# A four-layer cross-attention stack: the third layer's norms and gate by exp and ln, its experts joined at the gate, its maxima's products placed between other work

## The chip, the cores and the metric

One core of one Trainium2 chip. The metric is the device time of one execution in microseconds (us), and the time of a kernel is the median of its runs.

## The reference, cut to what matters

Sixteen sequences of 56 tokens (width 256) pass through four layers, and every layer attends to the same context of 1500 rows per sequence (width 128). Layer 0 is one attention with a sigmoid gate, layers 1 and 3 are attention with 16 heads and a GELU feed-forward, and layer 2, the third one, is what changes:

```python
vm = expert_mask(token_type_ids)[..., None]              # token picks expert v or l
x = rms_norm(hidden_states, ln_in_w)
mixed = jnp.where(vm, x @ v_qkv, x @ l_qkv)              # then causal self attention
hidden_states = residual + jnp.where(vm, ctx @ v_dense, ctx @ l_dense)
ci = rms_norm(hidden_states, ln_post_cross_w)
cq = heads(ci @ cq_w, NH, CHD)                           # 16 heads of 8
ck, cv = jnp.split(encoder_outputs @ ckv_w, 2, axis=-1)  # 1500 keys
cctx = sdpa(cq, ck, cv, causal=False)
hidden_states = hidden_states + cctx @ cdense_w
mi = rms_norm(hidden_states, ln_post_attn_w)
v_out = jax.nn.silu(mi @ v_gate) * (mi @ v_up) @ v_down
l_out = jax.nn.silu(mi @ l_gate) * (mi @ l_up) @ l_down
hidden_states = hidden_states + jnp.where(vm, v_out, l_out)
```

Inputs and results are fp32.

## The kernel before

The sixteen sequences form four groups of four (224 tokens, two tiles of 112). The program is a list of sixteen items, layer by layer and group by group: items 0 to 3 are layer 0, 4 to 7 layer 1, 8 to 11 layer 2, 12 to 15 layer 3. Of every item the attention over the context runs in front (`att0`, `att13`, `att2`), and beside it, as a Python generator `side` that is advanced one step at a time between the attention's rounds, run the end of the item before (`post...`: output projection, feed-forward) and the start of the item after (`pre...`: norm, projections, and in layer 2 the self attention). A scheduler then puts each engine's instructions in order by program order, priorities and its own estimates; each engine works through its own queue in that fixed order.

**Layer 2's cross attention** (`att2`) counts half sequences n = 0 to 31, eight for each group. Each has six rounds (`NR`), a round being 250 of the 1500 keys. For half sequence n a round does, on TensorE: `weights(n, r + 1)`, four products (L984) into two PSUM banks, of which ScalarE takes the exponential (L991, two instructions); and `sums(n, r)`, four products with the values (L1012). The softmax needs each row's maximum first, so `maxima(n + 1)` runs one half sequence ahead: twelve **links**, two in each round. A link is two products (L941) into one of two banks and a VectorE maximum over that bank (L947). Two links that follow each other use the two banks in turn, so the third link's products wait until the first link's maximum has been read out. After the twelfth link comes the **tail**: the maximum over the links (L950), a split into two parts (L952, L953), a TensorE transpose (L955) and a spread copy (L961), which `weights(n + 1, 0)` needs. `att2` advances the generator `look` of the links at set points of a round (`next(look, None)`), and runs its rest and the tail at the fourth round with raised priority; nothing fixes where the scheduler puts a link among the other products.

**Keys and values** (`keys_values`) of the next sequence are made in the same rounds, one step for every second half sequence: GpSimd subtracts neighbouring key blocks (L874, L875: one instruction over 1250 columns) and spreads the queries (L888: one over 896 columns), TensorE multiplies (L895, L904).

**Norms**: `rms_rstd` squares on ScalarE (L258), takes the square root there (L260), and the reciprocal on VectorE (L261); then come the scaling (L269) and the transposes (L220). It is used twice in `pre2`, once in `post2`, and in layer 0. ScalarE evaluates functions out of one loaded table, and an ACT_TABLE_LOAD stands in its queue wherever the next function is not in it: Exp, Sqrt and Silu are in three different ones, copies and squares in all.

**The feed-forward** (`post2`) goes expert by expert. The normed rows come twice, once masked for expert v and once for l. For each expert the whole gate and up weights are loaded (`load_w`, three buffers `w`), and for each of six column tiles gate and up products (L1152) share a bank, Silu reads it (L1156), VectorE multiplies (L1157). The down products (L1166) of both experts add up in one bank.

The link's code, and where a round advances it:

```python
for r in range(NR):
    for i, bank in enumerate(cross["scores"]):
        ...                      # two products (L941), one maximum (L947)
        yield
```

## Time and profile before

| what | value |
|---|---|
| median of three runs (lowest, highest) | 2965.62 us (2954.15, 2970.51) |
| the profiled execution: its own time, its span | 2950.62 us, 2948.8 us |
| busy: PE, PEld, DVE, ACT, POOL | 2756.1, 2035.4, 1497.3, 1257.6, 123.1 us |
| mean granted TensorE clock, whole span | 0.979 |
| layer 2's cross attention, 1084 to 2024 us: PE, DVE, ACT busy, clock | 811.27, 477.67, 392.76 of 940 us, 0.95 |
| layer 1 with its neighbours, 450 to 980 us: PE busy, clock | 528.77 of 530 us, 1.00 |
| layer 3, 2100 to 2948 us: PE busy, clock | 838.79 of 848 us, 1.00 |

PE is TensorE's matmuls, PEld its weight loads, DVE VectorE, ACT ScalarE, POOL GpSimd. A wait row reads "engine line <- engine line: us in total, times, longest"; a timeline row gives start, length, engine, line, operation, operands, how many, and in brackets the idle time ahead of it with what ended it.

### The profile page before, as it was taken

How to read it: one execution, taken by the hardware profiler on the slowest of the kernel's cores; microseconds unless marked ns; L12 is line 12 of the kernel's file. 1: busy time of each engine (PE TensorE's matmuls, PEld its weight loads, DVE VectorE, ACT ScalarE, POOL GpSimd, SP SyncE). 2: the span in 40 equal slices, each digit the busy share in tenths (PEclk: the TensorE clock that was granted, in tenths of full speed). 3: DMA queues.
4: the chain of work that ended last, by engine and by line, in shares of the span. 5: the costliest groups of instructions: out<-in, count | busy, mean ns of one | idle time of the engine just before them, and what ended most of it. 6: DMA issues, size and time to landing. Idle time of an engine off the chain costs nothing.

```text
span 2948.8 us, 39063 instructions
## 1 busy us (share of the span) xinstructions
PE 2756.1 (93%) x15546; PEld 2035.4 (69%) x15546; DVE 1497.3 (51%) x3660; ACT 1257.6 (43%) x2098; POOL 123.1 (4%) x118
## 2 busy tenths in 40 slices
PE   5899999999999999888888988989999999999998
PEld 3677777777777766556566655756777777777777
DVE  2445645546546544654455465355455555555553
ACT  1444444444444433346235334535345345344443
POOL 0000000000000000010001000000000000000000
PEclk8999999999999999999989989999999999999999
DMA  5221121121110133253324423441211111111100
GB/s 171 97 77 38 34 81 37 35 81 37 35 60 24 53 92 89 53 128 102 74 72 114 117 53 82 116 116 54 91 43 58 56 37 63 56 37 49 56 22 4
DMA packets 72139, 198.47 MB, mean 67 GB/s; under 512 B 7334, under 2 KB 39718, under 8 KB 71958
## 3 DMA queue, kind: packets, MB, share of 16 engines
q1 hardware_dynamic: 71958, 195.98, 23.0%
q8 instruction: 123, 2.02, 0.3%
q14 instruction: 58, 0.48, 0.1%
HBM read 145.88 MB, written 0.92 MB: 50 GB/s over the span
## 4 chain that ended last, share of the span: by engine, by line
PE 83%; DVE 10%; ACT 3%; issue 2%; DMA 1%; SPq 1%; DVEq 0%; ACTq 0%
PE o L344 19%; PE sc L305 19%; PE t L332 9%; PE o L1012 6%; DVE mx L947 3%; PE sc L941 3%; PE mm L1152 2%; PE t L984 2%; PE mm L690 2%; PE mm L661 2%; PE mm L571 2%; PE mm L677 2%; PE mm L1166 1%; PE t L593 1%; PE sc L904 1%
## 5 line engine op out<-in xcount | busy, mean ns | idle before, releaser
L344 PE MATMUL o<-pt,kv 125*128 125x256 f32 (+1 forms) x3072 | 661.2, 357 | 5.5 <-DVE pt L339 1.6
L344 PEld LDWEIGHTS o<-pt,kv 125*128 125x128 f32 x3072 | 519.9, 190 | 201.7 <-ACT pt L213 68.8
L305 PE MATMUL sc<-kt,qa 128*128 128x500 f32 x1344 | 635.2, 587 | 0.7 <-ACT qa L213 0.5
L314 DVE CUSTOM_DVE_ANT_0 p<-sc,mb 128x500 f32<-128x500 f32 x672 | 448.2, 673 | 214.2 <-PE sc L305 206.0
L321 ACT ACTIVATE p<-p,few 128x1500 f32<-128x1500 f32 x224 | 346.1, 1545 | 303.3 <-DVE few L319 302.7
L213 ACT ACTIVATE pt<-t 125x512 f32<-125x512 f32 x464 | 264.7, 590 | 374.1 <-PE t L332 351.8
L332 PEld LDWEIGHTS t<-ident,p 128*125 128x125 f32 x2688 | 356.8, 187 | 56.2 <-issue 15.4
L332 PE MATMUL t<-ident,p 128*125 128x128 f32 x2688 | 370.0, 273 | 2.1 <-DVE p L323 1.9
L947 DVE TENSOR_REDUCE mx<-sc 112x2 f32<-112x500 f32 x384 | 251.3, 674 | 200.4 <-PE sc L941 199.9
L305 PEld LDWEIGHTS sc<-kt,qa 128*128 128x128 f32 x1344 | 225.3, 190 | 135.3 <-issue 100.0
L991 ACT ACTIVATE pt<-t 125x448 f32<-125x448 f32 x384 | 192.3, 541 | 252.8 <-PE t L984 251.1
L339 DVE COPY pt<-t 125x512 f32<-125x512 f32 x224 | 154.3, 689 | 238.1 <-PE t L332 237.6
L941 PE MATMUL sc<-k,qs 128*112 128x250 f32 x768 | 188.9, 343 | 61.2 <-DVE mx L947 59.9
L323 DVE TENSOR_SCALAR p<-p,few 128x1500 f32<-128x1500 f32 x224 | 228.0, 1018 | 5.1
L941 PEld LDWEIGHTS sc<-k,qs 128*112 128x112 f32 x768 | 113.7, 184 | 123.8 <-DVE mx L947 88.7
L1012 PE MATMUL o<-pt,vc 125*64 125x224 f32 x1536 | 197.4, 387 | 0.3
L984 PE MATMUL t<-qs,k 128*125 128x224 f32 x768 | 146.0, 286 | 2.0 <-ACT pt L991 2.0
L322 DVE RECIPROCAL few<-few 128x1 f32<-128x1 f32 x224 | 36.0, 161 | 205.3 <-ACT p L321 205.3
L1012 PEld LDWEIGHTS o<-pt,vc 125*64 125x64 f32 x1536 | 101.1, 144 | 46.6 <-ACT pt L991 3.2
L984 PEld LDWEIGHTS t<-qs,k 128*125 128x125 f32 x768 | 120.1, 195 | 9.8 <-issue 4.0
L213 ACT ACTIVATE ot<-o 128x256 f32<-128x256 f32 (+1 forms) x128 | 45.4, 354 | 177.6 <-PE o L344 177.5
L120 POOL TENSOR_SCALAR mb<-m 128x1500 bf16<-128x1500 uint8 x32 | 46.9, 1465 | 1757.8 <-DVE few L314 1353.9
(272 smaller groups left out, 2724.2 us busy)
## 6 DMA issues: line engine op xcount, KB each, us to landing
kt<-in_ctxT SPq DMA_DIRECT2D x48, 750.0 KB
kv<-in_ctx SPq DMA_DIRECT2D x38, 750.0 KB
k<-kh SPq DMA_DIRECT2D x128, 187.5 KB
k<-kl SPq DMA_DIRECT2D x128, 187.5 KB
w<-in_L_W SPq DMA_DIRECT2D x16, 1024.0 KB
w<-in_L_Wq SPq DMA_DIRECT2D x8, 1024.0 KB
w<-in_L_Wo SPq DMA_DIRECT2D x8, 1024.0 KB
m<-in_mask_k SPq DMA_DIRECT2D x32, 187.5 KB
```

The source lines that it names most:

```text
L213: nc.scalar.activation(out, in_, AF.Copy, scale=scale)
L305: nc.tensor.matmul(sc[:n, :SW], qa[:, off : off + n], kt[:, cols], start=True, stop=True)
L314: nc.vector.tensor_tensor_reduce(p[:n, cols], sc[:n, :SW], mask[:n, cols], 1.0, LOWEST, ALU.add, ALU.max, mx[:n, s : s + 1],)
L321: nc.scalar.activation(p[:n], p[:n], AF.Exp, bias=nm[:n], accum_out=den[:n])
L323: nc.vector.tensor_scalar(p[:n], p[:n], den[:n], None, ALU.mult)
L332: nc.tensor.transpose(t[:CP, j * gw + off : j * gw + off + n], p[:n, c * CP : (c + 1) * CP], ident[:n, :n],)
L344: nc.tensor.matmul(o[:, :gw], kv[:, c, :], pt[:, j * gw : (j + 1) * gw], start=(c == 0), stop=(c == NC - 1),)
L941: nc.tensor.matmul(sc[:, e], made["q"][:, g, 2 * e : 2 * e + 2, :].rearrange("p h n -> p (h n)") .bitcast(F32R), k.bitcast(F32R), start=(r ...
L947: nc.vector.tensor_reduce(mx[:, 2 * i : 2 * i + 2, r], sc, AX.X, ALU.max)
L984: product = nc.tensor.matmul(t[:, i * T : (i + 1) * T], made["k4"][g][:, c * CP : (c + 1) * CP].bitcast(F32R), made["q"][:, g].rearrange(" ...
L991: nc.scalar.activation(pt[:, : 2 * T], t, AF.Exp)
L1012: av = nc.tensor.matmul(o[i * 64 : (i + 1) * 64, half * T : (half + 1) * T], made["v"][:, at : at + 64], pts[h][:, i * T : (i + 1) * T], s ...
```

## The change

Line numbers above and below are those of the kernel before. The change has six parts:

- `rms_rstd(x, ln=True)` in layer 2 takes Ln and then Exp with scale -0.5 in place of the square root, and one Newton step by five small VectorE instructions in place of the reciprocal.
- `post2` adds both experts' gate products in one bank (each token's rows are zero for the other expert), and likewise the up products. Silu becomes Exp, Ln, Exp on ScalarE and a VectorE product with the gate. Weights are loaded in halves of the columns, both experts in one buffer; the down products of the two experts go to two halves of a bank, and four VectorE instructions per group add them, weighted with the new table `takes`. That table is made once, at the end of layer 0's first item, by eight one-column products, a copy and one more instruction.
- Beside item 9 a table that holds both Exp and Ln is loaded ahead.
- GpSimd's subtraction runs in five instructions of 250 columns, its spread in four of 224.
- `maxima` yields ahead of a link instead of behind it, and each link is given the name of an instruction that its products must follow on TensorE (`look.send`, `behind`: an order, not a wait): the last of the next weights' products or the last of the sums' products.
- The points of a round at which `att2` advances the links move to behind `weights` and behind `sums`. Their number in a round stays.

```diff
...
@@ -188,6 +190,16 @@
         nc.vector.memset(vm, 0.0)
         nc.vector.tensor_mul(vm[:, :, : N - 1], is1v[:, :, : N - 1], is1v[:, :, 1:])
         nc.vector.tensor_scalar(nvm, vm, -1.0, 1.0, ALU.mult, ALU.add)
+
+        nc.vector.memset(share, 1.0 / 128)
+        p = mm()
+        vmf = vm.rearrange("p b n -> p (b n)")
+        for i in range(B * N // TP):
+            nc.tensor.matmul(
+                p[:TP, i : i + 1], vmf[:, i * TP : (i + 1) * TP], share, start=True, stop=True
+            )
+        nc.vector.tensor_copy(takes[:, 0], p[:TP, : B * N // TP])
+        nc.vector.tensor_scalar(takes[:, 1], takes[:, 0], -1.0, 1.0, ALU.mult, ALU.add)
@@ -251,19 +263,31 @@
             )
         return xT
-    def rms_rstd(x):
+    def rms_rstd(x, ln=False):
         ss = stat(NT)[:TP]
         sq = xpool.tile([TP, NT, D], F32, tag="xn", name="sq")
         for i in range(NT):
             nc.scalar.activation(sq[:, i, :], x[:, i, :], AF.Square, accum_out=ss[:, i : i + 1])
         rstd = stat(NT)[:TP]
-        nc.scalar.activation(rstd, ss, AF.Sqrt, bias=eps6[:TP], scale=1.0 / D)
-        nc.vector.reciprocal(rstd, rstd)
+        if ln:
+
+            nc.scalar.activation(rstd, ss, AF.Ln, bias=eps6[:TP], scale=1.0 / D)
+            nc.scalar.activation(rstd, rstd, AF.Exp, scale=-0.5)
+
+            v, t = stat(NT)[:TP], stat(NT)[:TP]
+            nc.vector.tensor_scalar(v, ss, 1.0 / D, 1e-6, ALU.mult, ALU.add)
+            nc.vector.tensor_mul(t, rstd, v)
+            nc.vector.tensor_mul(t, t, rstd)
+            nc.vector.tensor_scalar(t, t, -0.5, 1.5, ALU.mult, ALU.add)
+            nc.vector.tensor_mul(rstd, rstd, t)
+        else:
+            nc.scalar.activation(rstd, ss, AF.Sqrt, bias=eps6[:TP], scale=1.0 / D)
+            nc.vector.reciprocal(rstd, rstd)
         return rstd
     def rmsnorm_T(x, w, gi, masked):
-        rstd = rms_rstd(x)
+        rstd = rms_rstd(x, True)
         xn = xpool.tile([TP, NT, D], F32, tag="xn", name="xn")
         for i in range(NT):
             nc.vector.tensor_scalar(
@@ -351,6 +375,14 @@
         for _ in steps:
             pass
+    def behind(ins, name, why):
+
+        tc.add_manual_dep(
+            ins, name,
+            mybir.DependencyInfo(mybir.DependencyClass.NoSync, mybir.DependencyReason.DATA),
+            reason=why,
+        )
+
@@ -872,9 +904,10 @@
         else:
             kd = wpool.tile([128, 2048], F32, tag="w", name="kd")[:, :M]
         nc.gpsimd.tensor_copy(kd[:, : 2 * CP], kt[:, : 2 * CP])
-        nc.gpsimd.tensor_tensor(
-            kd[:, 2 * CP :], kt[:, 2 * CP :], kt[:, : M - 2 * CP], ALU.subtract
-        )
+        for c in range(2 * CP, M, 2 * CP):
+            nc.gpsimd.tensor_tensor(
+                kd[:, c : c + 2 * CP], kt[:, c : c + 2 * CP], kt[:, c - 2 * CP : c], ALU.subtract
+            )
         kh, kl = (big.tile([128, 2 * R], F32, tag="qa", name=n)[:, :M] for n in ("kh", "kl"))
         made["k"] = kh, kl
         vc = kpool.tile([CP, KV], F32, tag="kv", name="vc")
@@ -885,10 +918,11 @@
         qs = mpool.tile([128, 4, 4, N], F32, tag="mb", name="qs")
         made["q"] = qs
         cq = state["cq"][:, :, b % G * N : (b % G + 1) * N]
-        nc.gpsimd.tensor_tensor(
-            qs.bitcast(F32R), cq.unsqueeze(2).to_broadcast([128, 4, 4, N]),
-            m_four.unsqueeze(1).unsqueeze(3).to_broadcast([128, 4, 4, N]), ALU.mult,
-        )
+        for g in range(4):
+            nc.gpsimd.tensor_tensor(
+                qs[:, g].bitcast(F32R), cq[:, g].unsqueeze(1).to_broadcast([128, 4, N]),
+                m_four.unsqueeze(2).to_broadcast([128, 4, N]), ALU.mult,
+            )
         for s in range(NS):
             p = bank()
             cols = slice(s * SW, (s + 1) * SW)
@@ -933,19 +967,22 @@
         mx = small.tile([TP, 4, NR], F32, tag="mx", bufs=2, name="mx")
         for r in range(NR):
             for i, bank in enumerate(cross["scores"]):
+                at = yield
                 sc = bank[:TP, :SW].rearrange("p (e k) -> p e k", e=2)
                 g = n % 2 * 2 + i
                 k = made["k4"][g][:, r * 2 * CP : (r + 1) * 2 * CP]
                 for e in range(2):
-                    nc.tensor.matmul(
+                    product = nc.tensor.matmul(
                         sc[:, e],
                         made["q"][:, g, 2 * e : 2 * e + 2, :].rearrange("p h n -> p (h n)")
                         .bitcast(F32R),
                         k.bitcast(F32R), start=(r + e == 0), stop=True, skip_group_check=True,
                     )
+                    if at:
+                        behind(product.ins, at, "links between the others' products")
                 nc.vector.tensor_reduce(mx[:, 2 * i : 2 * i + 2, r], sc, AX.X, ALU.max)
-                yield
+        yield
         nm = few(4)[:TP]
         nc.vector.tensor_reduce(nm, mx, AX.X, ALU.max, negate=True)
...
@@ -1020,6 +1049,7 @@
                     if c == 0 and half:
                         behind(av, last[i], "groups of sums in a bank")
                     last[i] = av.name
+        return av.name
     def cross_own(o, out):
@@ -1062,6 +1092,13 @@
         steps = keys_values(gi * G, state)
         return steps if gi else run(steps)
+    def none():
+        while True:
+            yield
+
+    nothing = none()
+    next(nothing)
+
     def att2(gi, state, then, side):
         x = xs[gi]
         xf = x.rearrange("p i d -> p (i d)")
@@ -1080,7 +1117,7 @@
             ask(1)
             run(maxima(0))
             looks[1] = maxima(1)
-            for _ in range(2):
+            for _ in range(3):
                 next(looks[1])
         ready = cross.pop("ready", None)
         making = iter(())
@@ -1100,26 +1137,29 @@
                 pts = ready[0]
                 if r == NR - 1 and n + 2 < end:
                     looks[n + 2] = maxima(n + 2)
-                look = looks.get(n + 1 + r // (NR - 1), iter(()))
+                    next(looks[n + 2])
+                look = looks.get(n + 1 + r // (NR - 1), nothing)
                 if r == NR - 1:
                     ready = weights(n + 1, 0) if n + 1 < end else None
                 else:
-                    next(look, None)
                     ready = weights(n, r + 1)
+                    if r < NR - 2:
+                        look.send(ready[1])
                 next(side, None)
                 if not half:
                     next(making, None)
                 if r == 2 and n + 2 < end:
                     ask(n + 2)
-                next(look, None)
                 if r % 2:
                     next(side, None)
-                sums(n, r, pts, o, last, ready[1] if r < NR - 1 else None)
+                at = sums(n, r, pts, o, last, ready[1] if r < NR - 1 else None)
+                if r != NR - 2:
+                    look.send(at)
                 if r in (0, 2, NR - 1):
-                    next(look, None)
+                    look.send(at)
                 elif r == NR - 3:
                     with tc.high_priority(offset=200):
-                        run(look)
+                        next(look, None)
             if half:
                 cross_own(o, ccT[:, :, b * N : (b + 1) * N])
         cross["ready"] = ready
@@ -1134,42 +1174,53 @@
     def post2(gi, state):
         x = xs[gi]
-        xf = x.rearrange("p i d -> p (i d)")
         xe = rmsnorm_T(x, "L2_ln_post_attn_w", gi, True)
         yield
-        hs, downs = [], []
-        for n, e in enumerate("vl"):
-            (wg,) = load_w((a[f"L2_{e}_gate"], 2, I2))
-            (wu,) = load_w((a[f"L2_{e}_up"], 2, I2))
-            hT = big.tile([128, 8, T], F32, tag="hT", bufs=2, name="h2T")
-            for f in range(NF2):
-                cols = slice(f * 128, min(I2, (f + 1) * 128))
+
+
+        hT = big.tile([128, 8, T], F32, tag="hT", bufs=2, name="h2T")
+        for f0 in (0, NF2 // 2):
+            lo, hi = f0 * 128, min(I2, (f0 + NF2 // 2) * 128)
+            kinds = [
+                load_w(*((a[f"L2_{e}_{k}"][:, lo:hi], 2, hi - lo) for e in "vl"))
+                for k in ("gate", "up")
+            ]
+            for f in range(f0, f0 + NF2 // 2):
+                cols = slice(f * 128 - lo, min(hi, (f + 1) * 128) - lo)
                 w = cols.stop - cols.start
                 p = mm()
-                for k, wt in enumerate((wg, wu)):
-                    for c in range(2):
-                        nc.tensor.matmul(
-                            p[:w, k * T : (k + 1) * T], wt[:, c, cols], xe[n][:, c, :],
-                            start=(c == 0), stop=(c == 1),
-                        )
-                nc.scalar.activation(hT[:w, f, :], p[:w, :T], AF.Silu)
+                for k, experts in enumerate(kinds):
+                    for n, wt in enumerate(experts):
+                        for c in range(2):
+                            nc.tensor.matmul(
+                                p[:w, k * T : (k + 1) * T], wt[:, c, cols], xe[n][:, c, :],
+                                start=(n + c == 0), stop=(n + c == 2),
+                            )
+                    yield
+
+                s = tmp("silu")[:w, :T]
+                nc.scalar.activation(s, p[:w, :T], AF.Exp, scale=-1.0)
+                nc.scalar.activation(s, s, AF.Ln, bias=ones[:w])
+                nc.scalar.activation(s, s, AF.Exp, scale=-1.0)
+                nc.vector.tensor_tensor(hT[:w, f, :], p[:w, :T], s, ALU.mult)
                 nc.vector.tensor_tensor(hT[:w, f, :], p[:w, T : 2 * T], hT[:w, f, :], ALU.mult)
-                yield
-            hs.append(hT)
-            downs.append(load_w((a[f"L2_{e}_down"], NF2, D))[0])
-        p = mm()
+        downs = [load_w((a[f"L2_{e}_down"], NF2, D))[0] for e in "vl"]
         for i in range(NT):
+            p = mm()
             for n in range(2):
                 for f in range(NF2):
                     w = min(128, I2 - f * 128)
                     nc.tensor.matmul(
-                        p[:TP, i * D : (i + 1) * D], hs[n][:w, f, i * TP : (i + 1) * TP],
-                        downs[n][:w, f, :],
-                        start=(n + f == 0), stop=(n == 1 and f == NF2 - 1),
+                        p[:TP, n * D : (n + 1) * D], hT[:w, f, i * TP : (i + 1) * TP],
+                        downs[n][:w, f, :], start=(f == 0), stop=(f == NF2 - 1),
                     )
                 yield
-        nc.vector.tensor_add(xf, xf, p[:TP, : NT * D])
+            for n in range(2):
+                nc.vector.scalar_tensor_tensor(
+                    x[:, i, :], p[:TP, n * D : (n + 1) * D],
+                    takes[:, n, gi * NT + i : gi * NT + i + 1], x[:, i, :], ALU.mult, ALU.add,
+                )
@@ -1188,6 +1239,11 @@
         return items[k][1](items[k][4], states[k]) if k < len(items) else None
     def beside(k):
+        if k == 2 * groups + 1:
+
+            tc.keep_in_program_order(
+                nc.scalar.preload_act_table_set("natural_log_exp_and_others")
+            )
         if k:
             _, _, _, post, gi = items[k - 1]
             yield from post(gi, states.pop(k - 1))
```

## The prediction

> **What bounds the kernel now.** I read the page first: the totals, the clock in 40 slices, and the chain that ended last.
>
> ```profile
> span 2948.8 us, 39063 instructions
> ...
> PEclk8999999999999999999989989999999999999999
> ...
> PE 83%; DVE 10%; ACT 3%; issue 2%; DMA 1%; SPq 1%; DVEq 0%; ACTq 0%
> ```
>
> TensorE is the chain, except for a tenth that is VectorE's. Windows by stage, of which two rows follow (length, then busy time of PE, PEld, DVE, ACT, POOL, then the clock), say where that tenth lies.
>
> ```profile
> 1084.00:2024.00 940.00, 811.27 (x5257) 585.00 (x5257) 477.67 (x977) 392.76 (x713) 68.53 (x74) 0.95 0.37 93
> ...
> 1276.00:1281.00 5.00, 4.50 (x19) 3.67 (x21) 2.36 (x6) 1.95 (x5) 0.10 (x1) 0.73 0.82 279
> ```
>
> Layers 1 and 3 keep PE busy for 99% at clock 1.00. Layer 2's cross attention, 940 us, leaves it idle for 129 us and at a clock of 0.95. What PE waited for in that stage, in the waits:
>
> ```profile
> PE sc L941 <- DVE mx L947: 59.9, 75, 2.0
> PE sc L955 <- DVE nml L953: 20.8, 18, 2.0
> PE mm L220 <- DVE xn L269: 12.9, 6, 2.8
> PE mm L733 <- DVE s L729: 12.2, 8, 3.3
> ...
> PE t L984 <- ACT pt L991: 2.0, 5, 0.5
> ```
>
> Half of it is the links waiting for an earlier maximum; ScalarE, whose queue holds many table loads, is hardly waited for. One such link in the timeline:
>
> ```profile
> 1248.75 1.02 PE L941 MATMUL sc<-k,qs 128*112 128x250 f32 x4
> 1249.60 0.49 PE L984 MATMUL t<-qs,k 128*125 128x224 f32 x3
> 1250.88 1.26 DVE L947 TENSOR_REDUCE mx<-sc 112x2 f32<-112x500 f32 x2
> 1251.61 0.48 PE L941 MATMUL sc<-k,qs 128*112 128x250 f32 x2 [1.52 <-DVE mx L947]
> 1251.93 0.26 PE L984 MATMUL t<-qs,k 128*125 128x224 f32 x1
> ```
>
> Two links, three weights' products, and a third link that needs the first one's bank. It waits 1.52 us while a weights' product and four sums' products (0.98 us) that could run stand behind it. The second wait, the tail's, with its cause:
>
> ```profile
> 1293.85 1.68 POOL L888 TENSOR_TENSOR qs<-l,tables 128x896 fp32r<-128x896 f32 x1 [17.75 <-PE t L984]
> 1294.31 1.25 DVE L952 CAST nml<-few 112x4 fp32r<-112x4 f32 x1
> 1295.81 0.32 PE L955 MATMUL sc<-ident,nml 112*128 112x112 f32 x1 [2.04 <-DVE nml L953]
> ```
>
> The cast of 4 columns, usually 0.17 us, ends with GpSimd's spread. PE waits 2.04 us; at six like places without GpSimd it waits 0.96 to 1.05, at six with it 1.88 to 2.04.
>
> **The change part by part.** The sum is made against the profiled execution's own 2950.6 us (span 2948.8), which is 15.0 below the runs' median of 2965.6. Numbers of places come from the built order of instructions of both kernels, which holds no time.
>
> *Links.* The timeline's 59.9 us sort by what stands between two uses of a bank. "Two links, one or three weights' products, one link" has 28 places and costs 38.8 us; three or more links in a row cost 10.4 us, 0.36 for each of 29 links; "link, three weights' products, link" has 18 places at 0.25, 4.5 us; the rest is 6.2. In the changed order the first kind has 0 places in place of 29, because all four weights' products and four sums' products, 1.6 us, now come first. The runs of ten are gone and 13 runs of three links stay (13 x 0.4 = 5.2 us), 17 of the third kind (4.2), the rest I leave (6.2). New are some 22 places with one key product (L895, 0.5 us) and the other bank's link (0.49) between. A maximum on an idle VectorE was done 0.77 us after its products, so they wait 0 to 0.4 us; I take 0.15, since VectorE is half idle (3.3). 59.9 becomes 19: **-41** (bounds -28, if all of these wait 0.4 and runs 0.7, and -52).
>
> *Tail.* With only four weights' products (0.6 us) between the last link and L955, PE waits 1.05 us. Before, 12 tails stood so, six of them hit by GpSimd (about 2.0 each). In the changed order 24 do, because the links come later and the tail does not. 24 x 1.05 = 25 us, and 6 x 0.2 for the smaller GpSimd instructions (1.68 / 4 = 0.42 us each, so a cast meets half of one): 26.7 for 20.8, **+6** (0 to +14, if a queued maximum stands ahead as well).
>
> *GpSimd.* The subtraction (2.40 us) also held one L729 for 2.61 us instead of 0.62, and the 3.27 us wait of L733 ends there: **-2** (0 to -2).
>
> *Norms.* Before: load 1.28, Sqrt 0.29, reciprocal 0.17, 1.74 us. After: Ln and Exp 0.58 and four serial VectorE instructions of 0.165 (the fifth runs beside), 1.24 and three more hand-overs: 0.4 less. Where the joint table is not loaded it is two loads and 3.8 us, 2.1 more. Of the six waits of L220 three (1.75 each) keep their place, -0.4 each; two (2.44) get four sums' products (0.98) in front, -1.4 each; the first (2.83) gains 2.1 and loses 1.2 that GpSimd cost it. **-3** (-7 to +4; the norms beside layer 1 and layer 3 are covered there by attention at 99%).
>
> *Gates.* PE's products stay as many. In groups 0 and 1 ScalarE drops some 14 loads of 1.283 us and 12 Silu of 0.357, and takes 18 short instructions, 6.4 us: 16 us less each, but it is off the path, 4 us of waits for it in the stage: **0** (-4 to +2). In group 2 the built order has two loads in every tile again, since layer 3's first norm takes its Sqrt before; 14 loads for 16: the same. Group 3's feed-forward runs beside layer 3's attention with 16 loads for 8, and the products of its last four tiles stand in one row, each waiting for a bank that exp, load, ln, load, exp (3.64 us) and two products (0.78) release. PE needs 3.4 us for a tile: two waits of about 1 us, and 2.3 ahead of the last down products: **+4** (0 to +8).
>
> One rule speaks against these loads. The Trainium skill, ScalarE: Activation LUTs, section "Table sets: the hidden batching unit", says that ln followed by exp takes one table load, as one set holds both. The built order here holds 12 loads ahead of an Ln and 10 ahead of the closing Exp. By the rule the +4 would be 0 and the sum 4 lower.
>
> *The rest.* `takes`: eight one-column products (the nearest row, L742, has eight in 0.40 us, weight loads of 0.11 each) while PE waits for VectorE anyway: **+1** (0.5 to 2). Loads: the same bytes in 32 issues for 16; v_down moves behind eight key copies and next to l_down, whose buffer comes free at the sixth gate tile as before; PE waited 1.3 us for it: 0 (to +5). The last additions, four of 0.48 for one of 0.69 in each group, delay nothing. What `behind` holds back is only links; behind them wait maxima and the tail, counted above.
>
> *Given back.* Rounds get 4% shorter, and with them the cover of the side's chains (L733, L1049, L711, L789 and others, some 25 us of waits): **+6** (0 to +20).
>
> *Clock.* After the 2.83 us wait of L220 the clock was 0.73 for 5 us, and eight L838 took 2.68 us for 1.68. A clock of 0.955 over 940 us is 42 us lost at most; idle time falls by a third, and half of a product's time stretches: **-7** (0 to -20).
>
> A second rule. The Trainium skill, TensorE: Matmul & The Clock Gate, section "HAM oscillation — how this bites in real kernels", asks only for no idle gaps over about 3.4 us; the longest here is 3.27. By it the clock term would be 0, the sum 7 higher.
>
> Sum: -41 + 6 - 2 - 3 + 0 + 4 + 1 + 6 - 7 = -36. The profiled execution would take 2914.6 us, the median 2965.6 - 36 = 2930.
>
> **The rivals.** (1) *The waits only change place.* The chains beside the links (side attention, tail) end last as soon as links do not: tails +14, given back +20, clock 0, links -41 and the rest 0 give -7, 2958. For it: all those chains run on VectorE, which the changed links use at the same pace. Against: VectorE is busy for 478 of 940 us. 20%.
>
> (2) *Slower: links held behind late sums.* The order puts links behind the sums, and these wait for ScalarE's exponentials (0.54 us each). If a round's sums came late, PE would stand with runnable links behind them, in each of 192 rounds. At 0.45 us (the waits' longest for L991 is 0.5) that is 86 us: 2965.6 - 36 + 86 = 3015. It decides from (36 + 15) / 192 = 0.27 us per round. For it: groups 2 and 3 put loads ahead of exponentials. Against: between weights and their sums still lie about 3 us of products, and no sum's product waited for L991 (their weight loads, which run ahead, 3.2 us in all). 13%.
>
> (3) *More than the sum.* Links at -52, the clock at -20, no giving back: -70, 2896. 7%.
>
> That the change does not do what it says is in the forecast: the one table holds in two of four groups.
>
> **How the numbers follow.** The forecast has 60%. About 0.5%, 15 us, is what a measurement of this kernel tells from no change. Faster by more: 0.57 of the forecast, all of (3), a quarter of (1), 0.69. Within: 0.03 and 0.14, 0.17. Slower: 0.14, (2) and a remnant of (1). The range runs from between (3) and the sum of the best bounds (-80), 2888, up to 2975, short of the worst bounds (+20), and leaves out most of (2) and little else.
>
> **What would show it.** In the changed profile: L941's wait for the maxima near 19 us, the tail's near 27, casts under 0.5 us, the stage's clock above 0.96, table loads 96 for 125, and a few us of waits in front of the down products after 2000 us. Wrong would be: waits of the sums for L991 of over 20 us, or the idle time of the stage above 115 us with the links' wait gone.

## The result, and the profile after

The changed kernel takes 2957.97 us (median of 20 runs, 2946.50 to 2968.12) beside 2962.90 us for the kernel before on the same chips: a ratio of 0.9981, 95% interval 0.9969 to 0.9993. That is 5 us less, no change by the bound of 0.5%, where 36 less was forecast. It lands on the first rival's 2958, in part by luck, as the section on why the prediction was wrong shows.

The profiled execution took 2960.50 us, 2.5 above its median, at a granted clock of 0.976. The one profiled before took 2950.62, 12 below its median of 2962.90, at 0.979, where the middle value of 23 other runs of that kernel (beside e1) is 0.976. So the two profiles lie 10 us apart the wrong way round: waits can be compared between them, times at a slow clock hardly. Lines of the changed kernel are meant from here on: links L976 and L984, tail L987 to L998, self-attention's last multiplication and transposes L761 and L765, gates L1203 to L1207. First the page (span and chain):

```profile
span 2958.7 us, 39263 instructions
...
PE 79%; DVE 11%; ACT 6%; issue 1%; DMA 1%; SPq 1%; DVEq 0%; ACTq 0%
```

ScalarE's part of the chain has gone from 3% to 6%, although its busy time fell. Next two windows, the links' stage and the one behind it, where the last group's feed-forward runs beside layer 3:

```profile
1084.00:2024.00 940.00, 815.94 (x5275) 596.05 (x5274) 480.38 (x1013) 353.37 (x704) 82.95 (x172) 0.94 0.37 93
...
2024.00:2110.00 86.00, 77.15 (x348) 57.13 (x348) 38.51 (x112) 48.27 (x70) 1.44 (x1) 1.00 0.28 92
```

The second window in the kernel before:

```profile
2024.00:2110.00 86.00, 85.07 (x394) 64.08 (x393) 41.36 (x116) 39.50 (x64) 1.44 (x1) 1.00 0.27 91
```

In the first, ScalarE has lost 39 us of work and PE stands still for 124 us in place of 129, at a lower clock. In the second PE stands still for 8.9 us where before it stood for 0.9. What PE waits for in the stage:

```profile
PE sc L992 <- DVE nml L990: 32.5, 26, 3.0
PE mm L765 <- DVE s L761: 23.9, 12, 2.5
PE sc L976 <- DVE mx L984: 23.3, 59, 2.1
PE sc L1079 <- DVE rd L1073: 12.0, 12, 1.7
PE mm L232 <- DVE xn L293: 9.4, 4, 4.5
PE mm L821 <- DVE qk L817: 6.5, 6, 1.3
```

The fourth and the sixth of these rows in the kernel before:

```profile
PE sc L1049 <- DVE rd L1043: 4.9, 6, 1.2
PE mm L789 <- DVE qk L785: 1.4, 1, 1.4
```

The links' waits did fall, from 59.9 to 23.3 us. In their place stand the tail (20.8 before), the self-attention (12.2), the reciprocals L1073 (4.9) and the queries and keys L817 (1.4): some 36 us saved, some 36 us spent.

A second reading needs the time of each half sequence, from tail to tail. The first 24 went from 714.3 to 704.5 us. The last seven, which begin with group 2's feed-forward, went from 182.4 to 190.1.

### The profile page after: what moved, and what is told of

It reads as the page before. It is cut to its first block, busy times and chain, and to the rows that moved or that the text cites. A ratio compares the mean times of both kernels' runs of the same rounds, so it can differ in the third digit from the quotient of the medians.

```text
span 2958.7 us, 39263 instructions
## 1 busy us (share of the span) xinstructions
PE 2759.3 (93%) x15554; PEld 2043.8 (69%) x15554; DVE 1504.7 (51%) x3723; ACT 1232.2 (42%) x2105; POOL 138.0 (5%) x230
## 4 chain that ended last, share of the span: by engine, by line
PE 79%; DVE 11%; ACT 6%; issue 1%; DMA 1%; SPq 1%; DVEq 0%; ACTq 0%
PE o L368 18%; PE sc L329 18%; PE t L356 9%; PE o L1041 5%; DVE mx L984 3%; PE sc L976 3%; PE mm L1196 2%; PE mm L722 2%; PE mm L693 2%; PE mm L603 2%; ACT p L345 2%; PE t L1021 2%; PE mm L709 2%; PE t L625 1%; PE mm L1214 1%
## 5 line engine op out<-in xcount | busy, mean ns | idle before, releaser
L984 DVE TENSOR_REDUCE mx<-sc 112x2 f32<-112x500 f32 x384 | 252.2, 674 | 178.4 <-PE sc L976 177.4
L1028 ACT ACTIVATE pt<-t 125x448 f32<-125x448 f32 x384 | 192.6, 540 | 201.9 <-PE t L1021 188.5
L976 PE MATMUL sc<-k,qs 128*112 128x250 f32 x768 | 190.0, 342 | 24.6 <-DVE mx L984 23.3
L976 PEld LDWEIGHTS sc<-k,qs 128*112 128x112 f32 x768 | 112.9, 183 | 102.2 <-DVE mx L984 56.2
L1021 PE MATMUL t<-qs,k 128*125 128x224 f32 x768 | 137.1, 284 | 1.3 <-ACT pt L1028 1.2
L225 ACT ACTIVATE ot<-o 128x256 f32<-128x256 f32 (+1 forms) x128 | 45.4, 355 | 185.5 <-PE o L368 185.5
L1021 PEld LDWEIGHTS t<-qs,k 128*125 128x125 f32 x768 | 116.3, 195 | 7.1 <-ACT pt L1028 2.8
```

The source lines that it names most:

```text
L225: nc.scalar.activation(out, in_, AF.Copy, scale=scale)
L976: product = nc.tensor.matmul(sc[:, e], made["q"][:, g, 2 * e : 2 * e + 2, :].rearrange("p h n -> p (h n)") .bitcast(F32R), k.bitcast(F32R) ...
L984: nc.vector.tensor_reduce(mx[:, 2 * i : 2 * i + 2, r], sc, AX.X, ALU.max)
L1021: product = nc.tensor.matmul(t[:, i * T : (i + 1) * T], made["k4"][g][:, c * CP : (c + 1) * CP].bitcast(F32R), made["q"][:, g].rearrange(" ...
L1028: nc.scalar.activation(pt[:, : 2 * T], t, AF.Exp)
```

## The experiments

Ratios are to the kernel before, by the medians, with the 95% interval; 0.1% is 3 us. "Half sequences" are times between tails of the profiled execution. "Slow stretches" are runs of whole microseconds of the links' stage in which the granted clock is below 0.97.

**Two parts of the change, each alone and together.** First the links' order alone, on the kernel before:

```diff
+                at = yield
                 ...
+                    if at:
+                        behind(product.ins, at, "links between the others' products")
-                yield
```

> The kernel before with the new order of the links and nothing else: Silu, Sqrt norms, GpSimd's large operations and three separate takes stay as they were. T1 (covers change place: the links' waits lay over the side chains of the self-attention, the gate and the out-projection, and an emptied wait comes back inside the chain): the waits of the links' products fall from 60 us to 15 to 25, the waits at the transposes of the self-attention's scores rise from 12 to 20 to 25 and those at the query/key scores from 1 to 5 or more, and the time lies 0 to 15 us under the kernel before. T2 (the order is worth what was forecast, 25 to 36 us, and the slow feed-forward of groups 2 and 3, some 20 us, took it back): 25 to 36 us under the kernel before. T3 (the new order itself loses: tails that wait behind three maxima in a row): at or above the kernel before, with tail waits of 30 us and more.

Measured: 1.0017 (1.0004 to 1.0030), 5 us slower. PE's waits in the stage (links L950, tail L966, self-attention L741):

```profile
PE sc L966 <- DVE nml L964: 41.2, 27, 2.0
PE mm L741 <- DVE s L737: 25.6, 12, 3.3
PE sc L950 <- DVE mx L958: 21.5, 58, 0.7
```

No table load was touched here, and the waits moved all the same. The links' and the self-attention's waits moved as T1 named it, the tail's as T3 had it, and the time is T3's: the order alone loses. T2 in this form does not hold. Next, the change without the links' order:

```diff
-                look = looks.get(n + 1 + r // (NR - 1), nothing)
+                look = looks.get(n + 1 + r // (NR - 1), iter(()))
                 ...                          # and the old points of advance
```

> The changed kernel with the old order of the links: norms and gate by exp and ln, the joined experts, the GpSimd share and the single take stay. T2: the table loads in groups 2 and 3 put the gate's product on VectorE behind ScalarE in those groups, and the time lies 10 to 20 us above the kernel before, 15 to 25 above the changed kernel. T1 alone, with gates that cost nothing: within 5 us of the kernel before. If gates, norms and GpSimd's share bring something by themselves: 5 us or more under the kernel before, and then the order of the links is worth nothing or less.

Measured: 1.0061 (1.0043 to 1.0080), 18 us slower: T2's number. Its last seven half sequences take 197.0 us (182.4 before). Then GpSimd's small instructions, with the links' order and alone:

```diff
+        for c in range(2 * CP, M, 2 * CP):   # subtraction: 5 instructions for 1
+        for g in range(4):                   # spread: 4 instructions for 1
```

> The kernel before with the new order of the links and GpSimd's subtraction and spread in small instructions; gates, norms and takes stay old. With the links alone the 24 half sequences of groups 0 to 2 took 723.8 us (before 714.3, changed kernel 704.5), and tails beside the spread waited 2.0 us each. T4 (GpSimd's large instructions beside VectorE's small ones ate the links' gain: the new order puts the casts of more tails beside them): those half sequences fall to 700 to 710 us, the tail's wait from 43 us to 33, and the time to 10 to 20 us under the kernel before. Rival (GpSimd is worth the 2 to 8 us forecast, and the difference to the changed kernel lies in its gates): half sequences at 715 to 722 us, within 6 us of the kernel before.

> The kernel before with GpSimd's small instructions and nothing else. The six casts that took 1.1 to 1.3 us and the one multiplication of 2.6 us fall to 0.2 to 0.6: 6 times 1 us at the tails and 2 us at the self-attention, 5 to 8 us under the kernel before if all of it stands on the path; within 3 us if, as T1 has it, the side chains take the place of what is saved. If T4 is wrong and GpSimd brings its gain without the links' order too, 15 us or more under the kernel before.

Measured: 0.9914 (0.9896 to 0.9932) together, 25 us faster, and 0.9942 (0.9922 to 0.9961) for GpSimd alone, 17 us faster. For the pair T4's half sequences (702.9 us) and tail's wait (30.9) came, with 5 us more gain than it named. GpSimd alone lies beyond its 15 us mark, so most of its gain does not need the links' order, and T4's reason is at most a part of it. The order's own worth on top is 8 us, no more than its uncertainty. GpSimd's two parts separately, with the links' order:

> The kernel before with the links' order and GpSimd's subtraction of key blocks in five instructions; its spread of the queries stays one instruction of 1.68 us. The links alone gave 1.0017, links with both 0.9914. T4 (the tails' casts beside the spread are the loss: tail waits of 2.0 us and the slow clock behind them): nearly all of the gain is missing here, ratio 0.998 to 1.001, the tails' wait still at 40 us. Rival (the subtraction of 2.4 us, which holds the self-attention's multiplication for 2.6 us and makes a wait of 3.3 us, is the loss): 0.991 to 0.995.

> The kernel before with the links' order and GpSimd's spread of the queries in four instructions of 224 columns; the subtraction stays one instruction. T4: nearly all of the gain is here, ratio 0.991 to 0.995, the tails' wait near 32 us and their longest near 1.9. Rival: 0.998 to 1.001 with the tails' wait down but the self-attention's 3.3 us wait and the time unchanged.

Measured: subtraction 0.9990 (0.9976 to 1.0005), spread 0.9943 (0.9923 to 0.9964). The spread is the larger part. One tail in the timeline, with the links' order alone and then with the spread in four:

```profile
1652.72 1.68 POOL L896 TENSOR_TENSOR qs<-l,tables 128x896 fp32r<-128x896 f32 x1 [24.57 <-PE t L995]
1653.17 1.25 DVE L963 CAST nml<-few 112x4 fp32r<-112x4 f32 x1
...
1654.67 0.32 PE L966 MATMUL sc<-ident,nml 112*128 112x112 f32 x1 [2.04 <-DVE nml L964]
```

```profile
1644.10 2.11 POOL L897 TENSOR_TENSOR qs<-l,tables 128x224 fp32r<-128x224 f32 x4 [24.76 <-PE t L996]
...
1644.55 0.17 DVE L964 CAST nml<-few 112x4 fp32r<-112x4 f32 x1
...
1645.25 0.32 PE L967 MATMUL sc<-ident,nml 112*128 112x112 f32 x1 [1.23 <-DVE nml L965]
```

The cast takes 0.17 us in place of 1.25, and PE waits 1.23 us in place of 2.04. From e1 to e15 the median falls by 22 us, while PE's idle time in the stage falls by 9 (132.1 to 123.0). An estimate of what the clock adds stands below, under "The clock".

**Norms and gates**, each on top of links and GpSimd:

```diff
+        if ln:                               # e9: rms_rstd by Ln, Exp, Newton
...
+            (exp, ln, exp, two products)     # e10: post2 as in the change, takes
```

The joint table is loaded ahead beside item 9 in e9 too, in e10 not.

> The kernel with links and GpSimd changed (0.9914 of the kernel before), plus the norms by ln and exp with the Newton step; gates by Silu as before. T2 (the loss of 20 us between that kernel and the changed one lies in the gates' table loads): the norms cost 0 to 8 us, chiefly one new wait of some 2.5 us beside layer 1 and the slower clock behind it, ratio 0.990 to 0.995. Rival (the norms' serial VectorE steps and two-load norms are the loss): 12 us or more, ratio 0.9955 or above.

> The kernel with links and GpSimd changed, plus the joined gates by exp and ln and the single take; norms by Sqrt as before. Here a Sqrt stands in the middle of each group's half sequences, so the table with both Exp and Ln is lost more often than in the changed kernel. T2: the gates' chain of exp, load, ln, load, exp holds VectorE's queue in more groups, and the time is 20 us or more above links and GpSimd alone, ratio 0.998 or above. If the gates' loads are harmless and the norms are at fault: ratio under 0.994.

Measured: norms 0.9993 (0.9975 to 1.0010), gates 1.0047 (1.0030 to 1.0065). The kernel they were put on has 0.9914 and the whole change, with both, 0.9981. So norms alone cost 23 us, gates alone 39, both 20. Each half of the pair breaks the other's table: with Silu kept the norms load twice each (10 for Ln, 9 for Exp), with Sqrt kept the gates do (24 and 22), and VectorE's waits at the gate's product come to 103.3 us between 1084 and 2110 us (65.8 in the changed kernel). For the norms the expectation failed. One of them in e9's timeline:

```profile
1549.10 1.28 ACT L262 ACT_TABLE_LOAD   x1
...
1550.70 1.28 ACT L263 ACT_TABLE_LOAD   x1
...
1552.24 0.16 DVE L267 TENSOR_TENSOR stat<-stat 112x2 f32<-112x2 f32 x1 [2.81 <-ACT stat L263]
...
1553.88 0.45 PE L1067 MATMUL sc<-ident,rd 112*128 112x112 f32 x1 [4.38 <-DVE rd L1061]
```

The first Newton step stands at the head of VectorE's queue for 2.81 us, and behind it the reciprocals of the finished half sequence, for which PE waits 4.38 us. This happens again at 1803 us, and three norms make PE wait 3.96 to 4.47 us themselves. Now, in the changed kernel, a Sqrt beside the feed-forwards goes:

```diff
-            nc.scalar.activation(rstd, var, AF.Sqrt, bias=eps5[:TP])
+        if g == "L3_ln_q_g":
+            newton(rstd, var, 1.0, 1e-5, eps5)      # Ln, Exp, one Newton step
```

> The changed kernel with one more norm taken off Sqrt: the first norm of the third layer (1 of the norms that run beside the feed-forwards of groups 2 and 3) is done by ln and exp with one Newton step too, at five small VectorE operations a call, and the program then holds 68 table loads for the 96. T2: VectorE's waits for ScalarE at the gate's product fall from 48 us to 30 or less, the half sequences of the feed-forward of group 2 go back from 38.8 us to 33 or less, and the time is 12 to 25 us under the changed kernel. T1 with the loads harmless: within 4 us of the changed kernel, with the feed-forward of group 2 still at 36 us or more or its gain lost at the transposes of the self-attention.

Measured: 0.9944 (0.9929 to 0.9959), 11 us under the changed kernel. VectorE's waits for ScalarE at the gate's product over 1084 to 2024 us, the stretch of the expectation's 48, here and in the changed kernel:

```profile
DVE h2T L1218 <- ACT silu L1217: 28.3, 18, 4.1
```

```profile
DVE h2T L1206 <- ACT silu L1205: 47.9, 18, 8.3
```

Half sequences 24 and 25, in which group 2's feed-forward runs, fall from 38.9 and 38.7 to 33.3 and 32.9 us, and PE is idle for 0.03 us between 2024 and 2110. The waits came below the 30 that T2 named, the half sequences to its 33, and the time fell 1 us short of its 12. How one gate tile stops PE in the changed kernel:

```profile
1852.59 1.28 ACT L1204 ACT_TABLE_LOAD   x1
...
1854.38 1.28 ACT L1205 ACT_TABLE_LOAD   x1
...
1856.10 0.39 DVE L1206 TENSOR_TENSOR h2T<-mm,silu 128x224 f32<-128x224 f32 x1 [6.02 <-ACT silu L1205]
...
1858.26 0.29 PE L992 MATMUL sc<-ident,nml 112*128 112x112 f32 x1 [3.03 <-DVE nml L990]
```

PE did not wait for the gate. VectorE stood 6.02 us at the head of its queue for the gate, and behind it stood a link's maximum and the tail, for which PE waited 3.03 us. Without this order, with one table:

> The changed kernel with the third layer's first norm by ln and exp, and the old order of the links. With the links' order this kernel gave 0.9944. If the order is worth what it was beside GpSimd's change alone (0.3%): 0.996 to 0.999. If it is worth the 24 us that it was in the changed kernel: 1.001 to 1.004. If it is worth nothing without the table loads: 0.993 to 0.995.

Measured: 0.9978 (0.9962 to 0.9994), the first of the three. The links' waits without the order (e18) and with it (e3):

```profile
PE sc L979 <- DVE mx L985: 70.2, 86, 2.0
```

```profile
PE sc L988 <- DVE mx L996: 19.4, 57, 0.6
```

The order takes 51 us out of these waits, but PE's idle time in the whole execution falls by 19 only (202.2 to 183.2): the rest changed place. The order is worth 10 us here (0.9978 to 0.9944), near the 8 beside GpSimd. In the changed kernel it was worth 14 more (e2 to after). PE's idle time falls alike in both pairs (219.4 to 199.4 from e2 to after), but the middle clock of the runs goes from 0.9775 to 0.978 there and from 0.981 to 0.9775 here: by the estimate under "The clock" some 10 of the 14. One norm more:

```diff
-        rstd = rms_rstd(x, True)
+        rstd = rms_rstd(x, gi > 0 or w != "L2_ln_in_w")
```

> The changed kernel with the third layer's first norm by ln and exp (0.9944 of the kernel before), and with the very first norm of layer 2, which runs beside layer 1's last item, taken back to Sqrt and the reciprocal. If that norm's new wait (2.5 us at its transposes, 1.0 in layer 1's attention and the slow clock behind, 4 to 5 us before the first link) is its table loads and Newton step: the wait goes to 0 to 1 us, and the time falls by 3 to 6 us, ratio 0.992 to 0.9935. If it is the order of instructions that the new program got: unchanged, 0.9944.

Measured: 0.9922 (0.9901 to 0.9944). The time moved as hoped, though the interval touches 0.9944; the wait of 2.52 us stayed. It belongs to the second norm of that item, not to the first; what went is the 1.04 us wait in layer 1's attention. The edit did not test what it was meant to.

**Covers.** The tail a round later, on the changed kernel:

```diff
-                elif r == NR - 3:
+                elif r == NR - 2:
                     with tc.high_priority(offset=200):
-                        next(look, None)
+                        look.send(at)        # transposes behind this round's sums
```

> The changed kernel with each tail (largest link, cast, transpose, copies) one round later, between the sums of the last round but one, so that a whole round's sums lie between the last link's maximum and its use. If the tail's wait of 33 us is a loss of its own: it falls under 12 us, and the time is 12 to 25 us under the changed kernel. T1 (a wait taken away here opens another one behind it): the tail's wait falls, the waits at the other side chains or at the spread copy that the next half sequence's scores need rise by as much, and the time stays within 6 us. A third way is slower by 5 us or more: the copies of the tail land so late that the first scores of the next half sequence wait for them.

Measured: 0.9962 (0.9947 to 0.9978), 6 us under the changed kernel, the edge of T1's. The tail's wait for L990 fell from 32.5 to 10.7 us, and 7.3 us for ScalarE and 4.7 for the late spread copy came up at its place. With one table:

> The changed kernel with both: third layer's first norm by ln and exp, and the tails one round later. If what the two save lies at different places (slow feed-forwards of groups 2 and 3; tails of all groups), their gains add: 0.37% and 0.19% measured alone give some 17 us under the changed kernel by the medians, and 25 to 35 by the profiles (half sequences 894.5 to 862 us and 7 after the stage). If T1 holds for these too, the second saving is lost to the side chains: 11 to 14 us, no more than one table alone.

Measured: 0.9900 (0.9878 to 0.9922), 24 us under the changed kernel: the two add. That it is 7 us more than their sum lies within the uncertainty of some 10 us. The self-attention's chain cut short:

```diff
-        nc.vector.tensor_reduce(mx, s, AX.X, ALU.max)
-        nc.vector.tensor_tensor(s, s, mx..., ALU.subtract)
```

> The changed kernel without the maximum and its subtraction in the self-attention's softmax of the third layer (the softmax is then taken over the scores themselves, mathematically the same). In each of its 16 calls two VectorE instructions of 0.62 us and their hand-overs leave the chain that ends in the transposes of the scores. T1 (this chain sets the length of its stretch, 66.0 us in 12 places with 23.9 us of wait): the wait falls by 12 places times 1.3 to 1.5 us, to 5 to 9 us, and the time by 12 to 20 us. Rival (the wait there is only where idle time shows that TensorE would have somewhere else): the wait falls, the links' and the tails' rise by as much, and the time stays within 5 us.

Measured: 0.9952 (0.9935 to 0.9969), 9 us under the changed kernel, below the forecast 12. The chain's wait:

```profile
PE mm L762 <- DVE s L758: 16.6, 12, 1.7
```

It fell by 7.3 us, half as far as forecast, and the links' and tails' rose by nothing together (55.8 to 55.9), so what the chain gives back is not lost again. The twelve stretches that the expectation speaks of, from the scores' products to the transposes, take 45.4 us in place of 66.0: with a shorter chain the stretch is shorter. Half sequences of groups 0 to 2 shrank from 704.5 to 679.2 us, of which some 6.5 are idle time; the other 18.8 are the same products at a clock of 0.97 in place of 0.94. The execution had lost some 9 us ahead of the links.

**The clock.** Waits as TensorE's gaps, and the clock behind one (timeline, then windows: the clock is the third column from the end):

```profile
1233.52 0.98 PE L1041 MATMUL o<-pt,vc 125*64 125x224 f32 x8
...
1238.24 0.92 PE L765 MATMUL mm<-ident,s 112*56 112x112 f32 x4 [2.50 <-DVE s L761]
...
1239.73 3.25 PE L1041 MATMUL o<-pt,vc 125*64 125x224 f32 x16
```

```profile
1232.00:1237.00 5.00, 3.60 (x29) 2.67 (x28) 4.27 (x9) 1.99 (x4) 0.00 (x0) 1.00 0.01 3
1239.00:1244.00 5.00, 5.00 (x31) 2.90 (x31) 1.27 (x5) 1.57 (x3) 2.32 (x6) 0.50 0.00 0
```

After a wait of 2.5 us the clock is at half, and sixteen of the sums' products take 3.25 us, where eight took 0.98 ahead of it. Over the kernels before and after and e1 to e8, 50 of 73 waits of 2 to 3 us have such a stretch within 2 us, 40 of 114 waits of 1.5 to 2 us, 35 of 343 waits of 0.8 to 1.5. The changed kernel has 23 such stretches, the kernel before 18, e1 22, e5 16, e8 13; of waits of 1.5 us and more they have 25, 20, 28, 19, 21.

One execution says little on this, but every run's time and mean granted clock are on record. Between runs of one kernel 0.001 less clock goes with 2.3 to 3.0 us more time (straight lines through the changed kernel's 20 runs and five sets of 12 to 23 runs of the kernel before, correlations of -0.77 to -0.95). The middle clock of each kernel's runs, to be read with this estimate:

| kernel | clock | kernel | clock |
|---|---|---|---|
| before | 0.976 | after | 0.978 |
| e1, links | 0.975 | e9, links, GpSimd, norms | 0.9765 |
| e6, GpSimd | 0.980 | e10, links, GpSimd, gates | 0.976 |
| e5, links, GpSimd | 0.982 | e3, one table | 0.9775 |
| e15, links, spread | 0.9785 | e18, the same without links | 0.981 |
| e8, short chain | 0.981 | e11 | 0.987 |

So of e6's 17 us some 10 go with the clock, and of the 22 from e1 to e15 some 9.

Would filling the wait prevent the slow stretches?

```diff
+            if not c:
+                for _ in range(7):           # e17: 3, and only beside the links
+                    nc.tensor.matmul(t[:8, :TP], den, ident[:TP, :TP], start=True, stop=True)
```

> The changed kernel with 7 products of 112 columns more in each of the 16 self-attention calls, whose results are overwritten: they read the sums of the exponentials, so they can run only in the last 1.2 us of the wait in front of the transposes of the scores. The chain itself is as long as before. Clock theory (a wait of 2 us and more is followed by about 4 us at half the clock; 10 of the changed kernel's 23 slow stretches in the stage follow such a wait at these transposes): with the idle time cut in two by the products, slow stretches fall to 15 or fewer, and the time by 6 to 18 us, although about 1 us of work was added 16 times. Rival (the slow clock has another cause, the average load or the DMA traffic): slow stretches stay at 20 or more and the time is the same or up to 5 us longer.

> The changed kernel with 3 products of 112 columns more in each of the 12 self-attention calls that run beside the links, reading the sums of the exponentials, their results overwritten. By the run with seven they take 0.65 us a place, and end before the scaled scores are there. Clock theory: the added 12 times 0.65 us lie inside the wait, slow stretches fall from 23 to 18 or fewer, and the time is 3 to 15 us under the changed kernel (ratio to the kernel before 0.993 to 0.997). Rival (the slow clock does not depend on the wait): 22 or more slow stretches, and the time within 3 us of the changed kernel or above it.

Measured: 1.0046 (1.0028 to 1.0064) and 1.0017 (1.0000 to 1.0034), 19 and 11 us above the changed kernel, where 6 to 18 and 3 to 15 less had been expected. The seven products took 1.50 us a place and pushed the transposes back. The three took 0.73 to 1.28. Slow stretches fell to 16 and 15, close to what the clock theory had, but they were longer: 94 and 108 us of slow clock in all for 123. The runs' middle clock is 0.980 and 0.977, for 0.978. Filling did not pay, and whether a wait makes the clock fall or only comes with it stays open. These products use 8 columns of weights; wider ones were not tried.

**What points further.** Late tail and short chain with links and GpSimd, gates and norms old (e11), and with the change's gates and norms and one table (e12; its profile is not used):

> Links and GpSimd changed, gates and norms old, the tail one round later, and the self-attention's softmax without its maximum and subtraction. Alone these gave, against the kernel they were put on, 0.19% (late tail) and 0.29% (short chain) by the medians. Added to 0.9914: ratio 0.984 to 0.988, some 2910 to 2925 us. If the savings are lost to one another as T1 has it: 0.990 to 0.9914.

> The changed kernel with the third layer's first norm by ln and exp, the tail one round later and the short self-attention chain (without the maximum and its subtraction). One table with late tail gave 0.9900; the short chain adds 0.29% if it adds, so 0.985 to 0.988, and 0.989 to 0.990 if it is lost. Against the kernel with old gates (run beside it) T2 says that gates by one table, once no Sqrt breaks it, are worth within 0.3% of Silu either way: ScalarE was not what TensorE waited for.

Measured: 0.9794 (0.9769 to 0.9819), 2900.13 us, and 0.9801 (0.9777 to 0.9825), 2902.58 us. Both beat both kernels by about 2%, and by more than the sum of their parts: 0.984 to 0.988 and 0.985 to 0.988 had been expected. e11's waits in the stage:

```profile
PE sc L949 <- DVE mx L957: 19.8, 56, 0.9
PE mm L738 <- DVE s L734: 14.1, 11, 1.7
PE sc L965 <- DVE nml L963: 9.2, 13, 1.1
```

No wait of these is over 1.7 us any more. Half sequences 0 to 23 take 669.8 us at a clock of 0.98, with 8 slow stretches in the stage and 8 waits of 1.5 us and more. T2's last claim, that norms and gates with one table are worth within 0.3% of the old ones, came here (0.07%, uncertain by some 0.35%). But without late tail and short chain the same comparison, e3 with e5, is 9 us slower (0.9944 for 0.9914, uncertain by 7), so that it is not shown in general.

## Why the prediction was wrong, point by point

Its direction held; its size failed by a factor of seven. The steps that failed are *given back* (24 us of waits for 6) and *tail* (12 for 6), by which the links' gain was spent again; *gates* and *norms*, forecast with `takes` as +2 together and measured as +20; and *GpSimd*, -17 for -2. By the medians the 5 us are made of three sums:

| part | forecast | measured |
|---|---|---|
| GpSimd's small instructions | -2 | -17 alone (e6) |
| links with tail, given back and clock | -41 + 6 + 6 - 7 = -36 | -8 on top of these (e5 to e6), -10 with one table (e3 to e18), +5 alone (e1) |
| norms, gates, takes | -3 + 0 + 4 + 1 = +2 | +20 on top of both (after to e5) |

The differences are uncertain by 4 to 8 us each.

*Links.* The mechanism was right and its size nearly: 59.9 became 23.3 for the 19 forecast. From e18 to e3, where nothing else changes, links give 51 us less of waits.

*Tail.* +6 was too small: +12 in the changed kernel, +13 from e18 to e3. The price of 1.05 us held for tails with an idle VectorE. The bound of +14 named the reason, a queued maximum in front: tails behind three links in a row wait 1.23 to 1.75 us.

*Given back.* Among the waits this step failed most. I took 4% shorter rounds times 25 us of waits. But the chains' length, not the rounds', sets their waits: twelve stretches from the scores' products to the transposes took 65.4 us before and 66.0 after, while link waits inside them fell from some 15 to 3 us and the chain's own wait rose from 12.2 to 23.9. From e18 to e3, with nothing but the order between them, the same twelve go from 63.6 to 66.0, and in e8, with the chain cut, to 45.4. With L1073 and L817 that is 11.7 + 7.1 + 5.1 = 24, for 6. Rival (1) put +20 on this and +14 on the tail; it was the better reading of the stage, and I gave it 20%. That the median falls on its 2958 is luck: it had GpSimd, norms, gates and `takes` at nothing together, and they came to -17 and +20; and it had the clock at nothing.

*Clock.* Forecast -7, since idle time would fall by a third. The reason failed: in the stage it fell from 129 to 124 us, and over the whole execution it rose, from 192.7 to 199.4. Yet the runs' middle clock rose from 0.976 to 0.978, by the estimate above worth some 5 us: the size is near the forecast by luck, and as large as the whole gain, so that the other terms, -29 in the forecast, came to about nothing. By parts it goes up with GpSimd's small instructions (e6, e5) and down again with the new norms or gates on top (e9, e10). The two profiles show the reverse, PE busy for 3 us more between the first and the last tail and 25 waits of 1.5 us and more for 20, but there the kernel before is seen in a quick execution. Long waits go with a slow clock, and the sum of all waits does not tell how many are long: 75 link waits with a mean of 0.8 us became 59 with a mean of 0.4, sizes that rarely have a slow stretch behind them. The Trainium skill's TensorE: Matmul & The Clock Gate, section "HAM oscillation — how this bites in real kernels", allows gaps to about 3.4 us; in these traces most waits of 2 to 3 us stand in front of a slow stretch, so that the clock term is no zero either.

*Gates.* +4 priced group 3 alone and took group 2 for unchanged, since its loads stay as many. It did not ask what is queued behind them: before, one VectorE product followed one Silu; now VectorE waits for three functions and two loads, with links' maxima behind it. Group 2's two half sequences are 14 us longer than before and 11 longer than in e3, the last group's products in front of layer 3 about 8; between e3 and the changed kernel the medians differ by 11. The Trainium skill's ScalarE: Activation LUTs, section "Table sets: the hidden batching unit", has one set that holds both functions. In these runs that spared the loads only where no other function came between: 96 loads fell to 68 when one Sqrt of layer 3 went.

*GpSimd.* -2 counted the one long multiplication, and six casts under "tail". For idle time that was about right: in e6 PE's idle time in the stage is 5.5 us less than before (123.2 for 128.7). I left out the clock, 0.980 for 0.976, some 10 us by the estimate above: of the tails that waited 1.8 us or more, 4 of 6 before and 9 of 11 in e1 have a slow stretch behind them. I also left out that with the links' order more casts lie beside a spread (tail 41.2 us in e1 for 30.9 in e5).

*Norms.* Forecast -3; the waits of L232 in the stage fell by 3.5 us, as priced. But I priced two loads as 2.1 us on the norm's own chain, and not what the Newton step holds up on VectorE while it waits for them, as in e9's timeline. One wait became 4.47 us, a new one of 2.52 us came at 957 us beside layer 1, which I had called covered, and PE is busy 3.6 us less from 450 to 980 us. Without the new gates they cost 23 us (e9).

*Rival (2)* did not come: PE waited 1.2 us for L1028 in front of L1021, and in front of the sums for nothing. *Would be wrong* had named idle time above 115 us with the links' wait gone: it is 124. Of the signs of being right the 96 loads came, and casts under 0.5 us but for one of 1.10 us; the links' 19 us, the tail's 27 and a clock above 0.96 did not (23.3, 32.5, 0.94).

*Sums.* Some were added up wrongly, without moving the forecast: the links' bound of -28 is what would be left by its terms (the saving is 32), the tail's terms make 26.4 and not 26.7, the terms of rival (3) make -66 and not -70, and the best and worst bounds -84 and +27, not -80 and +20.

## What to carry to other kernels

A wait in front of one engine may be the cover of another engine's chain. Before pricing its removal, take the chain's whole length from the trace, from its first instruction to its last, and lay the bounding engine's work in the same stretch beside it: only the difference can be saved. When an operation is moved to an engine with a strict queue, price what stands behind it there, and count waits above 2 us by number, apart from the sum of waits. Read the clock from many runs of both kernels: one profile of each can point the wrong way. Change parts of a patch singly: here two helped by 25 us, and two cost 20.

## What the runs showed of the hardware

- A cast of 4 columns on VectorE, 0.17 us alone, took 1.25 us while one GpSimd instruction over 896 columns ran, and 0.17 us beside four of 224, though these took longer in all (2.11 us for 1.68).
- The granted clock goes to 0.50 for 3.4 us at a time, sometimes 6.8 or 10.2 (0.57 on average over four whole microseconds). In ten kernels 50 of 73 waits of 2 to 3 us had such a stretch within 2 us, but only 35 of 343 waits of 0.8 to 1.5 us. Which is cause and which effect is not shown.
- Between executions of one kernel (the changed one, 20 runs) the mean granted clock lies between 0.974 and 0.983 and the time between 2968 and 2946 us, with a correlation of -0.95.
- Seven products with 8 columns of weights were recorded as 14 instructions and took 1.50 us at most places, more than twice the four transposes behind them (0.57).
